# Rotary tables fetched a slot ahead, and a transpose moved in front of the next masks, in a six-layer local-attention transformer

## The chip, the cores and the metric

One Trainium2 core runs the whole program in one launch. The metric is device time in microseconds (us); the time before is a median of three runs. The profile and the trace are of one further, profiled execution. Engines: TensorE (PE; PEld is its weight load), VectorE (DVE), ScalarE (ACT), GpSimd (POOL) and SyncE (SP), which issues most DMAs.

## The reference

Four blocks in a row act on x of shape (4, 512, 128), each as `x = x + attention(layernorm(x)) * silu(ffn(layernorm(x)))`. The change lies in the "ffn" of the third block, which is itself a transformer ("the first transformer", prefix `l2`): six layers, 16 heads of 64, windows of 32 tokens.

```python
for i in range(DEPTH):                                   # 6
    x = attn_layer(shift_tokens(x), Wqkv[i], q_scale[i], k_scale[i], Wo[i]) + x
    x = ffn_layer(shift_tokens(x), ...) + x
# attn_layer
q = l2norm(q) * qs;  k = l2norm(k) * ksc
q = q * cos * scale + rotate_half(q) * sin * scale
k = k * cos * inv + rotate_half(k) * sin * inv
sim = 8 * q k^T over the own and the previous window, masked;  out = softmax(sim) v
```

## The kernel before

**Tables.** `cos*scale` and `sin*scale` do not depend on the layer, but `qs` and `ksc` do. For each layer two tables of 1 MB (i=1 for K, i=0 for Q) are fetched into one of three buffers (`tables`, L1613; DMA issued by ACT, L1617) and multiplied in place by the layer's column (two ACT scalings of 128x1024, L1620). `tables` is called where a table is first used, but neither the fetch nor the scaling is pinned, so the scheduler may move them. In the program as built, the K table of layer l+2 is fetched in the first slot of layer l+1, as soon as a buffer comes free, and its scalings stand among the GELUs of that slot on ACT's queue. The Q table of layer l+1 is fetched and scaled in the last slot of layer l.

**Slots.** Work is cut into slots: one per layer, batch row b (4) and half of the heads gp (2), so 48. In each slot three generators are merged by planned costs (the numbers that they yield): `queries_keys` for this slot (L1624), `attention` about one slot behind (L1864), `feed_forward` further behind (L1688). PE's order is then pinned to this merge order (`placed`, L128/L124 are the helpers that issue every transpose and matmul), and so are a few ACT instructions (Ln, Exp, Gelu).

**Pieces**, as PE sees them, with the names that the text uses:

- QK: two 128x512 matmuls of a projection; four per slot. Its PSUM buffer is read by ACT (square, L1650) and then by DVE (times table, L1652 and L1654); POOL adds (L1651, L1655).
- UNIT: `unit_length` (L1673), the sums of squares of K; ACT takes Ln (L1678) and Exp (L1679) in PSUM, DVE multiplies (L1681), and SP copies K into `l_qk`.
- SC: two mask matmuls and 64 small score matmuls of one unit (a pair of heads in each of four groups); DVE takes the maximum (L1788) and subtracts it into P (L1790), POOL scales P (L1792), ACT takes the exponential (L1795).
- TURN: eight transposes of P (`turn`, L1797); ACT copies the result to PT (L1804). WEIGH: 64 small matmuls of PT with V; DVE divides into On (L1833).
- BACK: eight transposes of On (`turn_back`); ACT copies them into OT (L1846). CLOSE: four matmuls of OT with Wo, cut in two halves with WEIGH between them; the second matmul reads the part of OT that the last BACK wrote. DVE adds to y (L1859).
- V: half of the values; ACT copies (L1753). LEN: small matmuls for the lengths of Q; ACT Ln and Exp (L1738, L1739).
- Feed-forward: mean, variance (L1697 to L1704), w1 with GELU (L1713), w2.

All PSUM tiles of this transformer come from one pool of four buffers; a piece waits until the buffer that it takes was read by its last user.

**Steps.** A batch row has two slots and four units. From one SC to the next is a step, and from the second layer on the four steps of a row repeat, named here by their feed-forward work. PE's order before:

```
MEAN  SC mean      BACK QK   CLOSE WEIGH CLOSE LEN TURN QK
VAR   SC variance  BACK UNIT V     WEIGH QK    V   TURN QK
W1    SC w1 (x6)   BACK QK   CLOSE WEIGH CLOSE LEN TURN QK
W2    SC           BACK UNIT V w2  WEIGH QK    V   TURN QK
```

Of the kernel before, what the change touches and what calls it, by code (L numbers as in the profile page):

```python
# [17 lines left out]
F32 = mybir.dt.float32  # L18
# [7 lines left out]
B, S, D = 4, 512, 128  # L26
# [1163 lines left out]
class _Transformer:  # L1190
# [68 lines left out]
    def tables(self, l, i):  # L1259

        if ("tab", l, i) not in self.weights:
            nc, pre = self.nc, self.pre
            tab = self.TB.tile([128, 2, 2, S], F32, name=pre + "_tab")
            nc.scalar.dma_start(tab, self.a["k_rot_" + pre][:, 4 * i : 4 * i + 4, :].rearrange("p (m h) s -> p m h s", m=2))
            for h in range(2):
                v = tab[:, :, h, :]
                nc.vector.tensor_scalar(v, v, self.col(l, 9 + 2 * i + h), None, ALU.mult)
            self.weights["tab", l, i] = tab
        return self.weights["tab", l, i]
# [328 lines left out]
class _Paired(_Transformer):  # L1598
# [11 lines left out]
        nc.sync.dma_start(hb[64:128, 1:S], y[64:128, 0 : S - 1])  # L1610
        return hb

    def tables(self, l, i):  # L1613
        if ("tab", l, i) not in self.weights:
            nc, pre = self.nc, self.pre
            tab = self.TB.tile([128, 2, 2, S], F32, name=pre + "_tab")
            nc.scalar.dma_start(tab, self.a["k_rot_" + pre][:, 4 * i : 4 * i + 4, :].rearrange("p (m h) s -> p m h s", m=2))  # L1617
            for h in range(2):
                v = tab[:, :, h, :]
                nc.scalar.mul(v, v, self.col(l, 9 + 2 * i + h))  # L1620
            self.weights["tab", l, i] = tab
        return self.weights["tab", l, i]

    def queries_keys(self, rows):  # L1624
        net, nc = self.net, self.nc
        self.shift[rows[0]] = self.moved(rows[0][1], "hb")
        late = None
        for n, (l, b) in enumerate(rows):
            hb = self.shift[l, b]
            hk = hb.rearrange("p (u s k) -> p s u k", s=2, k=self.W)  # L1630
            for gp in range(self.GP):
                w = self.part("qk", l, gp)
                if gp and n + 1 < len(rows):
                    self.shift[rows[n + 1]] = self.moved(rows[n + 1][1], "hb")
                before, made = None, {}
                for i in (1, 0):
                    tab = self.tables(l, i)
                    t = self.TP.tile([128, 2, 2, S], F32, name=self.pre + "_rot", bufs=3)
                    sums = []
                    for g in range(2):  # L1640
                        p = self.S2()
                        for h in range(2):
                            c = 128 * (4 * g + 2 * i + h)
                            o = p[:, h, :]
                            net.mm(
                                o.rearrange("p (s u k) -> p s u k", s=2, k=self.W) if i else o, w[:, c : c + 128],
                                hk if i else hb,
                            )
                        sq = self.TP.tile([128, 2, S], F32, name="sqp", bufs=4)
                        nc.scalar.activation(sq, p, AF.Square)  # L1650
                        nc.gpsimd.tensor_tensor(sq[:, 0, :], sq[:, 0, :], sq[:, 1, :], ALU.add)  # L1651
                        nc.vector.tensor_tensor(t[:, g], p, tab[:, 0], ALU.mult)  # L1652
                        m = self.TP.tile([128, 2, S], F32, name="rotp", bufs=2)
                        nc.vector.tensor_tensor(m, p, tab[:, 1], ALU.mult)  # L1654
                        nc.gpsimd.tensor_tensor(t[:, g], t[:, g], m[:, ::-1, :], ALU.add)  # L1655
                        sums.append(sq)
                        yield 1.72
                        if before:
                            made["k"] = yield from self.unit_length(*before)
                            before = None  # L1660
                    before = sums, t
                    if late:
                        yield 0.7
                        yield from self.lengths(*late)
                        late = None
                made["q"] = self.stack(t)
                self.made[l, b, gp] = made
                late = made, sums
                if gp and n + 1 == len(rows):
                    yield from self.lengths(*late)  # L1670
                yield None
# [192 lines left out]
    def attention(self, rows):  # L1864
        units = [dict(l=l, b=b, gp=gp, j=j) for l, b in rows for gp in range(2) for j in range(2)]
        yield from self.values(units[0])
        yield 5.5
        OT = None
        for i in range(len(units) + 2):
            if i % 2:  # L1870
                yield None
            u = units[i] if i < len(units) else None
            last = units[i - 1] if 0 < i <= len(units) else None
            older = units[i - 2] if i > 1 else None
            if u:
                if i % 2 == 0:
                    qk = self.made.pop((u["l"], u["b"], u["gp"]))
                else:
                    u["ve"], u["vo"] = last["ve"], last["vo"]
                self.weights_of(u, self.scores(qk, u["j"]), qk["r"])  # L1880
                yield 1.85
            if older:
                if i % 2 == 0:
                    OT = self.TP.tile([128, 4, S], F32, name=self.pre + "_OT", bufs=1)
                self.turn_back(older, OT)
            yield 0.9
            behind = iter((3.44,))
            if i % 2 == 0 and i + 2 < len(units):
                behind = self.values(units[i + 2])
            elif i % 2 and older:  # L1890
                behind = self.close(older, OT)
            yield from itertools.islice(behind, 1)
            if u:
                self.exponentials(u)
            if last:
                self.divide(last, self.weigh(last))
                yield 0.95
            yield from behind
            if u:
                self.turn(u)  # L1900
                yield 0.9


def _constants():
# [141 lines left out]
```

## Time and profile before

| what | value |
|---|---|
| median of three runs | 3774.01 us (3765.28 to 3774.3) |
| profiled execution, its time | 3785.04 us |
| profiled execution, its span | 3783.3 us |
| first transformer in the span | about 1580 to 3210 us |
| PE busy in the whole span | 3401.7 us (90%) |
| from 2100 to 2360 us: PE, DVE, ACT, POOL busy | 245.9, 180.3, 138.4, 141.0 of 260 us |

The profiled execution is 11.0 us longer than the median; sums are made in the profile and carried over as differences. A busy PE counts matmuls in flight, so idle time and the distance between starts say more than the share. In the views, "x<-y" is written tile and read tiles, a trailing "[t <-z]" is idle time and what ended it, and a line such as `ACT l_tab L1620 <- DMA ...: 24.7, 7, 5.7` is total wait, how often, longest.

### The profile page before, as it was taken

The page shows a single profiled execution, that of the slowest core. Times are in us where ns is not written, and L with a number is a line of the kernel's source. Part 1 is how long each engine was busy: PE and PEld are TensorE (multiplying, and loading weights), DVE is VectorE, ACT ScalarE, POOL GpSimd, SP SyncE. Part 2 cuts the span into 40 slices and gives each one's busy share as a digit, 9 for nine tenths or more (in the row PEclk, how much of TensorE's full clock was granted, in tenths as well). Part 3 has the DMA queues.
Part 4 walks back from the last instruction along what each step waited for, and adds up shares of the span by engine and source line. Part 5 has one row for each costly group of instructions (what it writes and reads, how often), then busy time and mean ns, then how long its engine had stood idle before and what let it go on. Part 6 is the DMA issues. An engine that isn't in the chain of part 4 may idle for free.

```text
span 3783.3 us, 108894 instructions
## 1 busy us (share of the span) xinstructions
PE 3401.7 (90%) x48517; PEld 1858.1 (49%) x48645; DVE 2187.5 (58%) x3133; ACT 1810.1 (48%) x2468; POOL 1345.3 (36%) x1136
## 2 busy tenths in 40 slices
PE   7787899989899998899999999999999999679887
PEld 4454455544444443455555555555555555445454
DVE  6675455510533533376677666676676776367764
ACT  2333566633233333455555545555555555345555
POOL 1101343400011112465555555555555553042220
PEclk7677999999989999999999999999999999889998
DMA  1000000010100000154544555445545553323221
GB/s 39 8 24 7 26 1 1 1 59 2 53 1 3 1 3 2 45 123 116 128 106 117 124 114 127 104 110 136 117 100 124 114 114 93 104 65 76 52 50 40
DMA packets 131267, 248.92 MB, mean 66 GB/s; under 512 B 31160, under 2 KB 48736, under 8 KB 123872
## 3 DMA queue, kind: packets, MB, share of 16 engines
q1 hardware_dynamic: 121744, 222.16, 24.9%
q10 hardware_dynamic: 8624, 19.29, 1.6%
q8 instruction: 384, 6.29, 0.7%
q0 software_dynamic: 432, 0.51, 0.1%
q14 instruction: 83, 0.68, 0.1%
HBM read 50.08 MB, written 5.54 MB: 15 GB/s over the span
## 4 chain that ended last, share of the span: by engine, by line
PE 63%; DVE 14%; ACT 11%; issue 7%; DMA 3%; POOL 2%; SPq 0%; POOLq 0%; DVEq 0%; ACTq 0%
PE S L124 42%; PE S L128 6%; PE M L124 5%; PE o L1113 4%; ACT l_P L588 3%; PE o L621 2%; DVE l_rot L1652 1%; DVE rotp L1654 1%; DMA l_tab<-in_k_rot_l 1%; ACT sqp L1650 1%; PE S L1023 1%; DVE l_P L1790 1%; DVE mx L1788 1%; DVE l_mx L1088 1%; ACT l_P L1135 1%
## 5 line engine op out<-in xcount | busy, mean ns | idle before, releaser
L1655 POOL TENSOR_TENSOR l_rot<-l_rot,rotp 128x1024 f32<-128x1024 f32 x192 | 452.5, 2357 | 174.5 <-DVE rotp L1654 166.8
L124 PE MATMUL S<-hb,l_wqk 128*128 128x512 f32 x896 | 439.8, 610 | 25.3 <-DVE hb L92 9.8
L1651 POOL TENSOR_TENSOR sqp<-sqp 128x512 f32<-128x512 f32 x192 | 245.3, 1278 | 488.9 <-ACT sqp L1650 480.1
L1652 DVE TENSOR_TENSOR l_rot<-S,l_tab 128x1024 f32<-128x1024 f32 x192 | 234.5, 1221 | 295.8 <-ACT sqp L1650 290.9
L128 PE MATMUL S<-core,l_P 128*128 128x128 f32 x1856 | 265.2, 288 | 40.5 <-ACT l_P L1437 16.5
L128 PEld LDWEIGHTS S<-core,l_P 128*128 128x128 f32 x1856 | 216.2, 146 | 135.9 <-issue 46.4
L124 PE MATMUL S<-l_KT,l_QT 32*128 32x256 f32 (+7 forms) x1536 | 250.3, 480 | 33.8 <-ACT l_P L1135 14.2
L1135 ACT ACTIVATE l_P<-S 128x1024 f32<-128x1024 f32 x160 | 156.7, 1022 | 258.3 <-PE S L124 258.3
L1139 POOL TENSOR_SCALAR_AFFINE_SELECT l_P<-l_P 128x256 f32<-128x256 f32 x256 | 99.4, 406 | 407.6 <-ACT l_P L1135 403.3
L1650 ACT ACTIVATE sqp<-S 128x1024 f32<-128x1024 f32 x192 | 196.3, 1023 | 95.6 <-PE S L124 92.8
L124 PE MATMUL S<-l_OT,l_wo 128*128 128x512 f32 (+1 forms) x512 | 224.0, 562 | 18.7 <-DVE ffu L1584 7.7
L1654 DVE TENSOR_TENSOR rotp<-S,l_tab 128x1024 f32<-128x1024 f32 x192 | 233.0, 1214 | 0.7 <-POOL l_rot L1655 0.7
L124 PE MATMUL S<-l_wv,hb 128*128 128x512 f32 x448 | 217.0, 607 | 15.7 <-DVE l_rot L1681 7.1
L124 PEld LDWEIGHTS S<-hb,l_wqk 128*128 128x128 f32 x896 | 154.4, 192 | 151.7 <-issue 119.1
L1088 DVE TENSOR_REDUCE l_mx<-S 128x2 f32<-128x768 f32 (+1 forms) x192 | 154.9, 863 | 126.3 <-PE S L1023 126.3
L124 PEld LDWEIGHTS S<-l_ve,l_PT 64*32 64x32 f32 (+1 forms) x6656 | 159.9, 108 | 96.4 <-issue 54.9
L124 PE MATMUL S<-l_vo,l_PT 64*32 64x64 f32 (+1 forms) x6656 | 187.6, 226 | 5.8 <-issue 5.8
L1792 POOL TENSOR_TENSOR l_P<-l_P,rq 128x1024 f32<-128x1024 f32 x96 | 182.6, 1902 | 27.9 <-DMA xT<-away_x 14.2
L124 PE MATMUL S<-l_ve,l_PT 64*32 64x64 f32 (+1 forms) x6656 | 184.8, 226 | 8.4 <-issue 7.5
L124 PE MATMUL S<-l_qk 64*32 64x64 f32 x12288 | 152.5, 226 | 34.1 <-issue 16.5
L1681 DVE SCALAR_TENSOR_TENSOR l_rot<-S,l_rot 128x1024 f32<-128x1024 f32 x96 | 113.1, 1219 | 101.9 <-ACT S L1679 97.8
L124 PEld LDWEIGHTS S<-l_qk 64*32 64x32 f32 x12288 | 132.7, 105 | 65.1 <-issue 58.7
(406 smaller groups left out, 6785.8 us busy)
## 6 DMA issues: line engine op xcount, KB each, us to landing
l_qk<-l_rot SPq DMA_DIRECT2D x896, 128.0 KB
l_ve<-l_vo SPq DMA_DIRECT2D x160, 256.0 KB
l_tab<-in_k_rot_l ACTq DMA_DIRECT2D x16, 1024.0 KB
l_ve<-l_vo SPq DMA_DIRECT2D x48, 192.0 KB
l_wqk<-in_l2Wqkv SPq DMA_DIRECT2D x12, 512.0 KB
l_wv<-in_l2Wqkv SPq DMA_DIRECT2D x12, 256.0 KB
l_wo<-in_l2Wo SPq DMA_DIRECT2D x12, 256.0 KB
hb<-xn SPq DMA_DIRECT2D x24, 128.0 KB
```

The source lines that it names most:

```text
L124: self.placed(self.nc.tensor.matmul(out, lhsT, rhs, start=start, stop=stop, **kw))
L128: self.placed(self.nc.tensor.transpose(out, in_, self.ident[:n, :n]))
L588: nc.scalar.activation(P[:, e, c : c + n], P[:, e, c : c + n], AF.Exp, bias=mn[:, i : i + 1], scale=-1.0, accum_out=rs[:, i : i + 1],)
L1088: nc.vector.tensor_reduce(mxv[:, bs, 2 * m + e, 3 - i], s[u][:, :, c : c + n], axis=AX.X, op=ALU.max)
L1113: nc.tensor.matmul(o[b // 2][x : x + 32, S - n : S], V[:, 4 * (m // 2) + i, 32 * b : 32 * b + 32], P[b // 2][:, b % 2, c : c + n], start=i ...
L1135: nc.scalar.activation(P[u], s[u], AF.Exp, scale=scale)
L1650: nc.scalar.activation(sq, p, AF.Square)
L1651: nc.gpsimd.tensor_tensor(sq[:, 0, :], sq[:, 0, :], sq[:, 1, :], ALU.add)
L1652: nc.vector.tensor_tensor(t[:, g], p, tab[:, 0], ALU.mult)
L1654: nc.vector.tensor_tensor(m, p, tab[:, 1], ALU.mult)
L1655: nc.gpsimd.tensor_tensor(t[:, g], t[:, g], m[:, ::-1, :], ALU.add)
L1792: nc.gpsimd.tensor_tensor(P, P, rq.unsqueeze(2).to_broadcast([128, 16, 64]), ALU.mult)
```

## The change

`tables` becomes `fetch` and `adapt`, both pinned to program order on ACT. The K table of layer l+1 is fetched at the start of slot (l, b=2, gp=1) and scaled at the start of (l, 3, 1); the Q table is fetched in (l, 3, 1) between the K and Q projections and scaled in (l+1, 0, 0) at the same point. In `attention`, `turn` of a unit no longer stands at the end of its own step, but directly in front of the next unit's masks, and its planned cost is added to the one of the scores.

```diff
-    def tables(self, l, i):
-        if ("tab", l, i) not in self.weights:
...
-            nc.scalar.dma_start(tab, self.a["k_rot_" + pre][:, 4 * i : 4 * i + 4, :].rearrange("p (m h) s -> p m h s", m=2))
-            for h in range(2):
-                v = tab[:, :, h, :]
-                nc.scalar.mul(v, v, self.col(l, 9 + 2 * i + h))
...
+    def fetch(self, l, i):
+        tab = self.TB.tile([128, 2, 2, S], F32, name=self.pre + "_tab")
...
+        self.net.placed(self.nc.scalar.dma_start(tab, src))
+    def adapt(self, l, i):
+        for h in range(2):
+            v = self.weights["tab", l, i][:, :, h, :]
+            self.net.placed(self.nc.scalar.mul(v, v, self.col(l, 9 + 2 * i + h)))
...
+                ahead = gp and l < rows[-1][0]
+                if ahead and b == B - 2:
+                    self.fetch(l + 1, 1)
+                if ahead and b == B - 1:
+                    self.adapt(l + 1, 1)
                 for i in (1, 0):
-                    tab = self.tables(l, i)
+                    if i == 0 and l and (b, gp) == (0, 0):
+                        self.adapt(l, 0)
+                    if i == 0 and ahead and b == B - 1:
+                        self.fetch(l + 1, 0)
+                    tab = self.weights["tab", l, i]
...
-        yield 5.5
+        yield 6.4
...
+                if last:
+                    self.turn(last)
                 self.weights_of(u, self.scores(qk, u["j"]), qk["r"])
-                yield 1.85
+            elif last:
+                self.turn(last)
+            yield 2.75
...
             yield from behind
-            if u:
-                self.turn(u)
-                yield 0.9
```

Since the costs that the merge sees are other ones, more than TURN moves. PE's order after, as the program is built:

```
MEAN  SC mean      QK   BACK CLOSE WEIGH CLOSE LEN   QK TURN
VAR   SC variance  UNIT BACK V     QK    WEIGH V     QK TURN
W1    SC w1 (x6)   QK   BACK CLOSE WEIGH CLOSE LEN   QK TURN
W2    SC           UNIT BACK w2 V  QK    WEIGH V     QK TURN
```

On ACT the square of the QK in front of BACK now stands ahead of the copy of OT, and UNIT's Ln, the copy of OT and UNIT's Exp follow each other in that order.

## The prediction

> **What bounds the kernel.** I read the page's engine shares first, then the windows of single steps in the first transformer, then what PE and ACT waited for there, and last the chain of waits and ACT's timeline at the places that the diff touches.
>
> ```profile
> span 3783.3 us, 108894 instructions
> PE 3401.7 (90%) x48517; PEld 1858.1 (49%) x48645; DVE 2187.5 (58%) x3133; ACT 1810.1 (48%) x2468; POOL 1345.3 (36%) x1136
> ```
>
> PE is the busiest engine by far. The next view has one step per line: start and end, length, busy time of PE, PEld, DVE, ACT, POOL, granted clock, DMA share, GB/s. They are MEAN, W1 at the first slot of a layer, VAR, an ordinary W1, and W2.
>
> ```profile
> 2047.00:2061.60 14.60, 14.04 (x356) 8.26 (x356) 10.23 (x12) 6.47 (x9) 11.31 (x7) 1.00 0.82 203
> 2078.60:2101.90 23.30, 20.60 (x366) 10.81 (x366) 12.40 (x17) 12.02 (x14) 11.82 (x8) 0.93 0.66 165
> 2134.60:2150.90 16.30, 15.16 (x296) 8.32 (x296) 12.16 (x12) 10.87 (x12) 6.89 (x5) 1.00 0.18 42
> 2150.90:2169.30 18.40, 18.25 (x367) 10.20 (x367) 12.45 (x17) 10.06 (x12) 11.84 (x8) 1.00 0.61 138
> 2169.30:2185.80 16.50, 16.35 (x301) 9.25 (x301) 12.65 (x13) 8.94 (x9) 7.18 (x5) 1.00 0.44 101
> ```
>
> An ordinary row takes 14.6 + 16.3 + 18.4 + 16.5 = 65.8 us, and PE is nearly always in work. W1 and W2 have PE idle for 0.15 us: whatever new wait falls there is paid in full. The W1 at the first slot of a layer is 4.9 us longer. What ended PE's idle times in the repeating part (1805 to 3137 us; total, times, longest), and the chain inside that long step (start, length, what):
>
> ```profile
> PE S L124 <- issue: 22.6, 34, 1.4
> PE S L124 <- DVE l_P L1790: 12.9, 32, 0.4
> PE S L124 <- DVE ffg L1714: 7.9, 4, 2.5
> PE S L124 <- DVE l_rot L1681: 6.2, 11, 0.6
> PE S L124 <- ACT l_OT L1846: 1.8, 2, 0.9
> ```
> ```profile
> 2078.67 7.09 DMA l_tab<-in_k_rot_l
> 2085.79 1.15 ACT l_tab L1620
> 2086.96 1.28 ACT L1713
> 2088.25 0.70 ACT ffg L1713
> 2088.97 0.76 DVE ffg L1714
> 2089.78 9.21 PE S L124 x147
> ```
>
> ACT stands at the scaling until the table has landed 7.09 us after its issue; the last GELU queues behind it, the gated product L1714 behind that, and PE waits for a PSUM buffer.
>
> **Part 1, the tables.** The fetch is now a slot (about 33 us) ahead of the scaling, so this wait goes. By step lengths: W1 at the first slot of layers 1 to 4 took 22.79, 23.36, 22.03 and 22.28 us against 18.32 in a quiet row, 17.2 us too much. VAR at the last slot of five layers, where the Q table was fetched and scaled, took 18.90, 16.97, 16.61, 17.31, 16.97 against 16.38, 4.9 too much. Together 22.0 us. Bounds: 17.2 if VAR's excess has other causes, and 30.6, all of DVE's idle time that ended with a table's DMA. What is late next in these steps is only what stands in the other rows.
>
> The four scalings (1.15 us each) per layer remain. K's pair, 2.3 us, is now ahead of the square in one MEAN step per layer; there ACT is busy for 6.5 of 14.6 us, and the CLOSE behind it waits anyway by part 2, so only about 0.1 us is left: 5 x 0.1 = 0.5 (with no cover 2.3 each, 11.5). Q's pair lies in a W2 step, where ACT has 7.6 us to spare: 0.
>
> The K fetch now meets a MEAN step with DMA share 0.82. Before, it lay in a step with 0.66. The fetch is waited for a slot later, but other transfers share its engines: the copies of Q that the next scores need, and PE's instructions, since the 34 waits on "issue" (22.6 us, 0.66 each) are PE waiting for no engine. Bounds: 0 if these copies' slack of some 5 us holds, and 10 if each of the five fetches adds three such gaps (5 x 3 x 0.66). Taken: 3.
>
> [...] No row of before has a table fetch in a MEAN step.
>
> **Part 2, the order.** I replay each step with the durations of one quiet slot (starts to next starts on PE: QK and V 1.72, BACK and TURN 0.9, one CLOSE matmul 0.86, UNIT, w1 and w2 as before). ACT at the end of w1, before:
>
> ```profile
> 2976.21 0.68 ACT L1713 ACTIVATE ffg<-S,l_cols 85x512 f32<-85x512 f32 x1 [1.03 <-PE S L124]
> 2976.91 1.28 ACT L1285 ACT_TABLE_LOAD   x1
> 2978.20 1.01 ACT L1846 COPY l_OT<-S 128x1024 f32<-128x1024 f32 x1
> 2979.11 1.03 ACT L1650 ACTIVATE sqp<-S 128x1024 f32<-128x1024 f32 x1
> ```
>
> PE's w1 ended at 2976.01. GELU, table load and the copy of OT ran while PE did BACK and QK, and CLOSE did not wait. Four steps, with t=0 at the end of the step's feed-forward work:
>
> - **W1.** PE does QK until 1.72, BACK until 2.6, CLOSE's first matmul until 3.46. ACT is ready at 2978.20, so 2.19; the square now comes first and the copy of OT starts 0.91 later, at 3.10, and ends at 4.11. With 0.15 to resume, CLOSE's second matmul starts at 4.26: 0.8 us of new wait. ACT then does the exponential L1795, which has time. 21 rows have it: +16.8.
> - **MEAN.** QK ends at 0; the square starts at 0.2, the copy of OT at 1.11 and ends at 2.12. PE: BACK until 0.9, CLOSE's first matmul until 1.76, second at 2.27: 0.5 of wait. In return the wait of CLOSE for DVE's L1790 goes (12.9 us, 32 times, 0.40 each), since more PE work now lies between the subtraction and the reuse of its buffer. Net 0 (-0.1 to +0.1 a row).
> - **W2.** The order of PSUM buffers changes. The second-last QK takes the buffer of the QK only three tiles back. DVE frees it 3.53 us after that QK's end (square 0.2, L1652 at 1.26, L1654 until 3.53) plus 0.15; WEIGH entered from QK and V take 1.57 + 1.82 = 3.39. Wait 0.3: 21 x 0.3 = +6.3. With a third user of the same kind the wait would be a whole 1.2; with V's copy earlier, 0.
> - **VAR.** This step is a locked chain from the end of the QK in front of its masks (t=0, 3018.3 in the slot below): DVE's two table products end at 3.53, maximum and subtraction at 6.0, the feed-forward's parts (L1704) at 7.4, then Ln, Exp, and L1681, whose end at 11.86 lets the second V start:
>
> ```profile
> 3025.66 1.07 ACT L1678 ACTIVATE S<-S,l_tiny 128x1024 f32<-128x1024 f32 x1
> 3026.76 1.01 ACT L1679 ACTIVATE S<-S 128x1024 f32<-128x1024 f32 x1
> ```
> ```profile
> 3027.80 2.36 DVE L1681 SCALAR_TENSOR_TENSOR l_rot<-S,l_rot 128x1024 f32<-128x1024 f32 x2 [2.89 <-ACT S L1679]
> ```
>
>   Before, V started at 11.99 and V, TURN and QK (1.72 + 0.9 + 1.72) followed: 16.3. After, OT's copy (0.91) stands between Ln and Exp, so V starts at 12.9, and V, QK and TURN follow until 17.2; but the masks at the step's start come 0.9 after t=0, since a TURN stands there too: 16.3 again, net 0. If the chain doesn't begin early, because the SC that DVE waits for now comes behind that TURN, it costs 0.9 x 21 = +19; if the wait for L1681 (6.2 us in all) went, -6.
> - **TURN** in front of the masks needs the exponential L1795 of the unit behind, done long before. It has no row in this place; the nearest are TURN in front of QK (0.93 against 0.87 elsewhere) and WEIGH, which costs 0.16 when entered from wide matmuls. Bounds 0 and 0.16 x 84 = 13; taken 0, since TURN's count and neighbours of 128 columns stay.
> - **Rows of the first layer without feed-forward** (3): about 0.8 each, +2.4.
>
> **Sum.** -22.0 + 0.5 + 3 + 16.8 + 0 + 6.3 + 0 + 2.4 = +7.0 us. The profiled execution would be 3785.04 + 7 = 3792, and the median, which is 11.0 lower, 3774.0 + 7 = 3781.
>
> **Rivals.**
>
> *The copy of OT is late in all 48 CLOSE passages (slower).* If ACT reaches the square late everywhere, CLOSE's second matmul waits for a square and a copy less one matmul: 1.01 + 1.02 - 0.86 = 1.17. 48 x 1.17 = 56, less 12.9 for L1790, plus 6.3 for W2, less 22: +27, so 3801. It decides as soon as OT's copy ends more than 0.86 us after BACK. For it: the two waits that PE already had for L1846 (0.9 at most). Against: in MEAN ACT is idle for more than half.
>
> *The new waits are hidden (faster).* If the scheduler's order leaves ACT ready before QK ends, or if the waits eat idle time that PE had anyway ("issue", 22.6 us), only the tables remain: 3774 - 22 = 3752; with the waits for L1790 and L1681 gone too (12.9 + 6.2), 3733. For it: both are real rows. Against: W1 has no idle time that could swallow 0.8.
>
> *The change does not do what it says* (no gain from tables, as the scheduler brings them together again): fetch and scaling are both pinned, some 40 ACT instructions apart, so I leave it out.
>
> **How the numbers follow.** The forecast has 0.55, the slower rival 0.20, the faster 0.25. A measurement here can tell about 0.3%, 11.3 us, so "same" is 3763 to 3785. The forecast's own spread (3766 to 3796, from the table's bounds, the fetch's 0 to 10, and W2's and TURN's ends) lies 0.33 in same, 0.20 above and 0.02 below. The slower rival gives 0.18 to slower and 0.02 to same, the faster 0.23 to faster and 0.02 to same. Faster 0.25, same 0.37, slower 0.38. The range 3752 to 3804 leaves out the faster rival's lower half (about 0.12) and the slower rival's upper part (0.08).
>
> **What would show it.** Right: ACT's wait for the table's DMA is gone; W1 at a layer's first slot falls to about 19.1 like all others; a new row "PE <- ACT l_OT" of about 0.8 in W1 and 0.5 in MEAN; W2 at 16.8, VAR at 16.4, MEAN at 14.6; the row for L1790 gone. Wrong: W1 stays at 18.3, or VAR grows by the 0.9, or "issue" rises in the MEAN steps with a fetch.

## The result, and the profile after

The changed kernel takes 3805.6 us (median of five, 3801.9 to 3815.05) against 3774.3 of the kernel before in the same series: ratio 1.0085, 95% interval 1.006 to 1.011. It is slower by 31 us, where +7 was forecast, and 1.6 us beyond the end of the range. The two profiled executions lie 27.2 us apart (spans 3810.5 and 3783.3).

The page of the changed kernel shows hardly more PE work in a longer span, at the same share:

```profile
span 3810.5 us, 108883 instructions
PE 3421.3 (90%) x48645; PEld 1864.7 (49%) x48645; DVE 2202.4 (58%) x3133; ACT 1798.2 (47%) x2470; POOL 1347.8 (35%) x1136
```

The windows of single steps of the changed kernel, in the columns of before (start and end, length, PE, PEld, DVE, ACT, POOL busy, granted clock, DMA share, GB/s): an ordinary MEAN, VAR, W1 and W2, the W1 at the first slot of a layer, and a MEAN with a K fetch.

```profile
3028.00:3042.70 14.70, 14.42 (x358) 8.45 (x356) 10.41 (x12) 6.01 (x9) 9.40 (x6) 1.00 0.69 151
3042.70:3059.00 16.30, 14.86 (x298) 8.57 (x296) 12.17 (x12) 10.66 (x13) 9.01 (x6) 1.00 0.18 41
3059.00:3078.10 19.10, 18.54 (x368) 10.05 (x367) 12.83 (x17) 9.97 (x13) 9.81 (x8) 1.00 0.64 142
3010.90:3028.00 17.10, 16.93 (x303) 9.37 (x301) 12.66 (x13) 8.79 (x10) 9.18 (x5) 1.00 0.40 93
2093.70:2113.50 19.80, 18.95 (x369) 10.24 (x368) 12.82 (x17) 11.35 (x15) 9.81 (x8) 1.00 0.71 157
1706.10:1729.50 23.40, 17.46 (x359) 9.51 (x357) 10.43 (x12) 6.07 (x9) 9.35 (x6) 0.85 0.62 145
```

The first three lines are the forecast almost to the digit: 14.7, 16.3, 19.1. W2 is 17.1 where 16.8 was forecast. The fifth is 3.5 us shorter than its counterpart of before. The last was not forecast: PE is idle for 6 of 23.4 us, and the granted clock is 0.85. The same step took 16.7 us before.

What ended PE's idle times in the repeating part of the changed kernel (total, times, longest):

```profile
PE S L124 <- DVE l_rot L1694: 26.1, 20, 1.4
PE S L124 <- issue: 24.8, 27, 2.6
PE S L124 <- ACT l_OT L1859: 15.7, 36, 0.6
PE S L124 <- DVE rotp L1667: 2.3, 11, 0.2
```

The old row for P's subtraction (12.9 us) is nearly gone, as is ACT's wait of 24.7 us for the table's DMA. New are OT's copy (L1859), UNIT's product L1694, for which V waits in the locked VAR, and L1667, which frees the PSUM buffer of W2's last QK.

A step can be laid beside its twin of before, since both kernels have the same 94 steps in the same order. Step lengths (start of masks to start of the next masks), summed by kind from the two traces:

| steps | count | before | after | difference | forecast |
|---|---|---|---|---|---|
| MEAN with the K fetch | 5 | 77.7 | 92.2 | +14.5 | +3 |
| other MEAN (five with K's scaling) | 17 | 258.2 | 258.4 | +0.2 | +0.5 |
| VAR at the last slot of a layer | 5 | 86.8 | 86.3 | -0.5 | -4.9 |
| other VAR | 17 | 278.0 | 276.4 | -1.7 | 0 |
| W1 at the first slot of a layer, and other W1 | 22 | 424.5 | 426.3 | +1.8 | -17.2 + 16.8 |
| W2 | 21 | 356.5 | 365.0 | +8.5 | +6.3 |
| steps without feed-forward | 7 | 101.5 | 104.2 | +2.7 | +2.4 |
| until the first step | | 1599.6 | 1601.9 | +2.3 | 0 |

The last row is no effect of the change: in the kernels below the first step began anywhere from 1590.1 to 1602.3 us. The rest sums to +25.5, 18.5 above the forecast: 11.5 of it in the MEAN steps with the K fetch, 2.7 in VAR, 2.2 each in W1 and W2.

**What the long MEAN steps wait for.** Step by step they took 23.4, 19.2, 15.9, 18.1 and 15.6 us. In the first of them ACT issues the K table at 1703.19; the trace's table packets run from 1704.29 to 1709.41. PE's timeline in the changed kernel then has this line (idle before it and what ended it in brackets):

```profile
1712.76 0.44 PE L124 MATMUL S<-l_qk 64*32 64x64 f32 x8 [4.64 <-issue]
```

"issue" says that no engine released PE. The DMA queues of the changed kernel say what was missing; first from 1704.2 to 1709.9, then from 1709.9 to 1712.8 us (packets, MB, share of 16 engines; q10 carries the table, q1 the copies that SP issues):

```profile
q10 hardware_dynamic: 144, 1.05, 67.4%
q1 hardware_dynamic: 240, 0.39, 31.3%
```
```profile
q1 hardware_dynamic: 239, 0.68, 107.0%
q8 instruction: 1, 0.02, 2.9%
```

While the table moves, no packet of q8 runs; this queue, of the kind "instruction" and with packets of 16 KB, is taken for PE's by the pattern that follows. The next one starts at 1710.01, 0.6 us after the table's last, ends at 1711.36, and PE goes on 1.40 us later. In none of the five steps does a q8 packet begin during the K table's transfer (4.4 to 5.2 us), and none of PE's idle times over 0.1 us there ends with a copy's landing. That PE goes on behind a q8 packet is a pattern: in all 70 waits on "issue" over 0.4 us in the transformer in the two traces, PE went on between 1.21 and 1.71 us after the end of a q8 packet (medians 1.39 and 1.43).

The gap is then paid twice, since the granted clock behind it is 0.50. The window right after it in the changed kernel:

```profile
1713.10:1718.40 5.30, 5.30 (x10) 2.08 (x7) 2.45 (x2) 0.60 (x1) 0.00 (x0) 0.50 1.02 217
```

At a granted clock of 0.50 the QK there takes 3.41 us where it takes 1.72 elsewhere.

**POOL's order in the same steps.** Not all of the 14.5 us is the transfer's. POOL is not pinned, and in these five slots, in the changed kernel alone of all kernels here, the sum of squares (L1664) stands ahead of P's scaling (L1805). In the third of the steps:

```profile
2276.13 1.27 POOL L1664 TENSOR_TENSOR sqp<-sqp 128x512 f32<-128x512 f32 x1 [0.80 <-ACT sqp L1663]
2277.36 1.90 POOL L1805 TENSOR_TENSOR l_P<-l_P,rq 128x1024 f32<-128x1024 f32 x1
```
```profile
2283.45 1.02 PE L124 MATMUL S<-hb,l_wqk 128*128 128x512 f32 x2 [1.25 <-DVE l_On L1846]
```

In the other MEAN steps P's scaling comes first: it starts 5.3 us into a quiet step, and 7.2 us into this one. So the exponential, DVE's division L1846 and with it the PSUM buffer of the last QK come later. This step has no wait on "issue" over 0.1 us; its excess is this wait. Three of the five steps have it (1.06, 1.25 and 0.33 us), 2.6 us in all.

### The profile page after: what moved, and what is told of

It reads as the page before. It is cut to its first block, busy times and chain, and to the rows that moved or that the text cites. A ratio compares the mean times of both kernels' runs of the same rounds, so it can differ in the third digit from the quotient of the medians.

```text
span 3810.5 us, 108883 instructions
## 1 busy us (share of the span) xinstructions
PE 3421.3 (90%) x48645; PEld 1864.7 (49%) x48645; DVE 2202.4 (58%) x3133; ACT 1798.2 (47%) x2470; POOL 1347.8 (35%) x1136
## 3 DMA queue, kind: packets, MB, share of 16 engines
q1 hardware_dynamic: 121744, 222.16, 24.7%
## 4 chain that ended last, share of the span: by engine, by line
PE 62%; ACT 14%; DVE 13%; issue 7%; POOL 2%; DMA 2%; SPq 1%; POOLq 0%; ACTq 0%; DVEq 0%
PE S L124 42%; PE M L124 5%; PE S L128 4%; PE o L1113 4%; ACT l_P L588 3%; PE o L621 2%; ACT sqp L1663 2%; ACT l_OT L1859 2%; DVE l_rot L1694 1%; DVE l_rot L1665 1%; DVE rotp L1667 1%; PE S L1023 1%; DVE l_mx L1088 1%; ACT l_P L1135 1%; DVE mx L1801 1%
## 5 line engine op out<-in xcount | busy, mean ns | idle before, releaser
L1664 POOL TENSOR_TENSOR sqp<-sqp 128x512 f32<-128x512 f32 x192 | 245.7, 1280 | 410.2 <-ACT sqp L1663 395.4
L128 PE MATMUL S<-core,l_P 128*128 128x128 f32 x1856 | 262.6, 286 | 38.9 <-ACT l_P L1437 16.7
L124 PE MATMUL S<-l_KT,l_QT 32*128 32x256 f32 (+7 forms) x1536 | 250.9, 481 | 34.2 <-ACT l_P L1135 14.5
L124 PEld LDWEIGHTS S<-hb,l_wqk 128*128 128x128 f32 x896 | 164.8, 193 | 216.8 <-issue 177.1
L124 PE MATMUL S<-l_OT,l_wo 128*128 128x512 f32 (+1 forms) x512 | 233.9, 569 | 33.0 <-ACT l_OT L1859 22.6
L1667 DVE TENSOR_TENSOR rotp<-S,l_tab 128x1024 f32<-128x1024 f32 x192 | 233.3, 1215 | 0.8 <-POOL l_rot L1668 0.8
L1805 POOL TENSOR_TENSOR l_P<-l_P,rq 128x1024 f32<-128x1024 f32 x96 | 182.5, 1901 | 39.9 <-DVE l_P L1803 31.1
L1694 DVE SCALAR_TENSOR_TENSOR l_rot<-S,l_rot 128x1024 f32<-128x1024 f32 x96 | 113.2, 1220 | 126.7 <-ACT S L1692 125.5
L124 PEld LDWEIGHTS S<-l_vo,l_PT 64*32 64x32 f32 (+1 forms) x6656 | 158.5, 107 | 16.6 <-issue 16.5
```

What stands on the lines that cost most here:

```text
L124: self.placed(self.nc.tensor.matmul(out, lhsT, rhs, start=start, stop=stop, **kw))
L128: self.placed(self.nc.tensor.transpose(out, in_, self.ident[:n, :n]))
L1694: nc.vector.scalar_tensor_tensor(t[:, g], p[:, g, :].unsqueeze(1).to_broadcast([128, 2, S]), 1e12, t[:, g], ALU.min, ALU.mult)
L1805: nc.gpsimd.tensor_tensor(P, P, rq.unsqueeze(2).to_broadcast([128, 16, 64]), ALU.mult)
```

## The experiments

Ratios are to the kernel before on the same chip. Step sums of each kernel's trace stand in the table at the end of this section. In all of them theory A is that the K fetch in MEAN delays PE's instructions and that the order has its own price; the rivals are named in the expectations.

**Tables alone and order alone.** Each is one half of the diff: `tables_only` has `fetch` and `adapt` with the attention of before, `order_only` the new attention with the tables of before.

> The new fetch and adapt, with the old attention (TURN at the end of its step, old costs). Theory A (the K fetch in the MEAN step keeps PE's instructions waiting there, and the order has its own cost): the W1 steps at layers' first slots lose 4 us each (about -17), VAR about -1 to -5, but the MEAN steps with a fetch still grow by about 14 in all: 3768 us (3760 to 3776). Rival B (the long MEAN steps come from the new order, not from the fetch): no long MEAN steps here, 3753 us.

> The new attention (TURN in front of the masks, costs 6.4 and 2.75), with the old tables. Theory A: W1 +0.87 and W2 +0.55 in each of about 21 rows (30), early steps +3, VAR -1: 3806 us, and no MEAN step over 17 us. Rival B (long MEAN steps belong to the order): 3820 us, with the long MEAN steps at some layers. If the order costs nothing, 3774.

Measured: `tables_only` 3785.2 us, ratio 1.0011 (0.9996 to 1.0026); `order_only` 3802.4 us, 1.0063 (1.0042 to 1.0083). The long MEAN steps are in `tables_only` (20.5, 17.0, 16.7, 16.2, 18.3) and none is in `order_only` (14.7 to 15.7): rival B falls. `tables_only` does shorten the first W1 steps by 15.8 us; 11 of it is given back in the MEAN steps with the fetch. Theory A explains only a part of these 11: in each of the five PE's QK waits 1.10 us for OT's copy (5.5 us), which it does there neither before nor in `tables_later`; two of them have 6.8 and 3.4 us at a clock of 0.50; the waits on "issue" are 4.8 us in sum, as before (4.7). The time also missed the 3760 to 3776 that was expected, since VAR gave back only 0.9 us and K's scaling costs 1.0 us in each of its five MEAN steps (15.7 where a quiet one takes 14.66): with the old order PE's QK waits 1.05 to 1.21 us there for L1667, whose square stands behind the scaling on ACT. The order costs 24 us, 8 less than I had expected: W1 and W2 are as long as expected, but its first W1 steps, still with the old tables, are 5.9 shorter than before (20 to 21 us instead of 22 to 23). The new order hides part of the old wait, so the halves don't add up in the first W1 steps. In the medians they do within the noise (4 and 24 us against 31).

**The K fetch half a slot later.**

```diff
-                if ahead and b == B - 2:
-                    self.fetch(l + 1, 1)
...
                 for i in (1, 0):
+                    if i == 0 and ahead and b == B - 2:
+                        self.fetch(l + 1, 1)
```

> The changed kernel, but the K fetch is issued in front of the Q projections of the same slot, which is at the end of the MEAN step, so that it lands in VAR, where the DMA share was 0.18. Theory A: the MEAN steps with a fetch fall back to about 15.3 us, 14 in all, VAR pays 0 to 3: 3793 us. Rival C (the issue gaps wander and have nothing to do with the fetch): unchanged, 3805 us.

Measured: 3794.6 us, ratio 1.0039 (1.0027 to 1.0052), 0.46% or 17 us less than the changed kernel. The five MEAN steps fell from 92.2 to 75.0, and the other VAR steps paid 3.7 in sum. The same step as above, in this kernel:

```profile
1704.30:1720.60 16.30, 14.67 (x359) 8.41 (x357) 10.58 (x12) 5.95 (x9) 9.40 (x6) 1.00 0.66 148
```

It is 16.3 us instead of 23.4, at full clock. Rival C, gaps that wander without cause, falls.

**A dose.** The fetch is cut in two halves, one for each 32 columns of a head (cosines and sines of both), the second in front of the Q projections.

```diff
+        if l and i:
+            self.net.placed(self.nc.scalar.dma_start(tab[:, :, 0, :], src[:, :, 0, :]))
+            self.rest = tab, src
...
+                    if i == 0 and ahead and b == B - 2:
+                        tab, src = self.rest
+                        self.net.placed(self.nc.scalar.dma_start(tab[:, :, 1, :], src[:, :, 1, :]))
```

> The changed kernel, the K fetch cut in two: half of the table at the start of the slot, the other half in front of the Q projections. A dose: if PE's instructions wait behind the table's packets for as long as these last, half the bytes cost half, MEAN steps with a fetch 85 us instead of 92.2, 3799 us; if there is a slack that half a table fits into, they fall to 75 and the time to 3792; if the place or the issue on ACT costs, not the bytes, 3806.

Measured: 3799.7 us, ratio 1.0048 (1.003 to 1.0065). The MEAN steps take 92.2 with the whole table, 79.8 with half of it, 75.0 with none: half the bytes cost 28% of the excess. So it is not the issue on ACT, which still stands there; but as a dose this is rough. All of it lies in two of the five steps (19.1 and 16.2), POOL's order is the usual one again here and in `fetch_later`, which alone takes 2.6 us off, and the interval of the time overlaps that of `fetch_later` and that of the changed kernel.

**BACK ahead of QK again.** The total of the planned costs stays; TURN stays in front of the masks.

```diff
-            yield 2.75
+            yield 1.85
...
                 self.turn_back(older, OT)
-            yield 0.9
+            yield 1.8
```

> The changed kernel with the same total of planned costs, 0.9 of it moved from in front of BACK to behind it, so that PE does BACK ahead of QK and UNIT again and ACT copies OT ahead of the square; TURN stays in front of the masks. Theory A: the waits for OT's copy (18.8 us in the trace) go, W1 falls to about 18.4, and since the copy no longer stands between Ln and Exp the second V of VAR starts 0.9 earlier, VAR 15.4: together -38, 3768 us; with VAR unchanged 3787. Rival (the copy is not what CLOSE waits for, or another release is as late): 3805 us.

Measured: 3768.1 us, ratio 0.9972 (0.9953 to 0.999), against 1.0085 for the changed kernel: 1.13% or some 43 us less, as the two spans have it too (3766.7 and 3810.5; 39.5 of it from the first step on). PE's order is the new one, but with BACK in front of QK and UNIT. ACT at the end of w1, first in the changed kernel with what PE did for it, then in `back_first`:

```profile
3067.12 1.28 ACT L1285 ACT_TABLE_LOAD   x1
3068.41 1.02 ACT L1663 ACTIVATE sqp<-S 128x1024 f32<-128x1024 f32 x1
3069.33 1.01 ACT L1859 COPY l_OT<-S 128x1024 f32<-128x1024 f32 x1
```
```profile
3070.39 1.12 PE L124 MATMUL S<-l_OT,l_wo 128*128 128x512 f32 x2 [0.56 <-ACT l_OT L1859]
```
```profile
2960.71 1.01 ACT L1859 COPY l_OT<-S 128x1024 f32<-128x1024 f32 x1
2961.62 1.03 ACT L1663 ACTIVATE sqp<-S 128x1024 f32<-128x1024 f32 x1
```

In the changed kernel OT's copy follows the square and CLOSE's second matmul stands for it; with the copy first, CLOSE ran through. The windows of a VAR and a W1 step in `back_first`:

```profile
2935.70:2951.20 15.50, 14.91 (x298) 8.61 (x297) 12.16 (x12) 10.83 (x13) 8.98 (x5) 1.00 0.19 44
2951.20:2969.60 18.40, 18.40 (x369) 10.25 (x368) 12.65 (x17) 10.00 (x13) 9.85 (x9) 1.00 0.62 139
```

W1 is back at 18.4, and VAR fell from 16.3 to 15.5: its chain is shorter now that no copy stands between Ln and Exp, while TURN's move lets it begin early. W2 (372.8 in all) became longer still: a quiet one takes 17.0 (17.1 in the changed kernel), but PE met more waits on "issue" (gaps over 0.06 us in the trace: 14.9 us in W2 against 8.1). The K fetch is still in the MEAN steps, 90.4 us.

**The two cures together, and no fetch at all.** `both` is `back_first` with the fetch of `fetch_later`. `no_fetch` is `back_first` in which layer l+1's table is scaled out of layer l's, by the quotient of the two columns.

```diff
-            v = self.weights["tab", l, i][:, :, h, :]
-            self.net.placed(self.nc.scalar.mul(v, v, self.col(l, 9 + 2 * i + h)))
+            c = self.ratio[:, l - 1, 2 * i + h : 2 * i + h + 1] if l else self.col(l, 9 + 2 * i + h)
+            self.net.placed(self.nc.scalar.mul(tab[:, :, h, :], old[:, :, h, :], c))
```

> back_first (0.9 of the planned cost behind BACK) with the K fetch at the end of the MEAN step as in fetch_later. Theory A: the five MEAN steps with a fetch, 90.4 us in back_first, fall to about 75, VAR pays 0 to 3: 3753 us, 15 below back_first (3768). Rival C (issue gaps wander): 3768.

> back_first without any table fetch after the first: each layer's table is scaled out of the layer's before, by the quotient of the two columns (ten quotients more at the start; the scales must not be zero). Theory A: MEAN steps as in both, and VAR at the last slots loses the 1.6 us that one Q fetch took: 3751 us. If the fetches cost nothing wherever they stand: as back_first, 3768.

Measured: `both` 3759.5 us, ratio 0.9941 (0.9921 to 0.9961); `no_fetch` 3750.2 us, 0.9917 (0.989 to 0.9944). The MEAN steps are 74.9 and 74.0. `back_first` and `both` are the cleanest pair for the fetch, since in these steps both have P's scaling first on POOL and OT's copy ahead of the square on ACT. Of the 15.5 us between them, the waits on "issue" make 8.9 (12.4 against 3.5); the rest is, as an estimate, half of the 13.2 us that `back_first` runs there at a clock of 0.50, with none in `both`, since the QK above took 3.41 us instead of 1.72 at that clock. The times of the two overlap in their intervals, and 3753 had been expected of `both`. In `both` two VAR steps at last slots still take 19.6 and 19.2, with the Q fetch issued in front of them; in `no_fetch` all five take 15.5 or 15.6. Both beat the kernel before and the changed one.

**The old order with the later fetch.**

> tables_only (old attention) with the K fetch at the end of the MEAN step. Theory A: MEAN steps with a fetch fall from 88.8 to about 76, the first W1 steps keep their gain of 16: 3771 us. If the whole gain of 22 that the prediction gave to the tables is there: 3756. If the fetch costs as much in VAR: 3785.

Measured: 3768.9 us, ratio 0.9968 (0.9952 to 0.9985). The tables alone, well placed, bring 12 us, not 22: the first W1 steps gain 15.5, the five MEAN steps with K's scaling lose 3.7 (1.0 each against a quiet one), and VAR at the last slots gains 2.1.

Step sums in us, worked out as above:

| kernel | MEAN, K fetch (5) | VAR, last slot (5) | W1, first slot (5) | other W1 (17) | W2 (21) | other VAR (17) |
|---|---|---|---|---|---|---|
| before | 77.7 | 86.8 | 108.8 | 315.7 | 356.5 | 278.0 |
| after | 92.2 | 86.3 | 97.8 | 328.5 | 365.0 | 276.4 |
| `tables_only` | 88.8 | 85.9 | 93.0 | 314.9 | 358.3 | 277.6 |
| `tables_later` | 75.8 | 84.7 | 93.3 | 316.4 | 359.2 | 278.2 |
| `order_only` | 76.6 | 90.7 | 102.9 | 328.1 | 364.2 | 276.6 |
| `fetch_split` | 79.8 | 87.4 | 98.7 | 328.3 | 367.8 | 277.3 |
| `fetch_later` | 75.0 | 84.7 | 96.7 | 328.3 | 365.6 | 280.1 |
| `back_first` | 90.4 | 79.2 | 94.5 | 315.2 | 372.8 | 263.9 |
| `both` | 74.9 | 85.4 | 94.6 | 318.4 | 371.6 | 266.4 |
| `no_fetch` | 74.0 | 77.7 | 93.3 | 315.6 | 370.1 | 263.0 |

## Why the prediction was wrong, step by step

- **The replayed order was right.** W1's new wait for OT's copy was put at 0.8 us, and a quiet W1 is 0.87 longer; `back_first`, which puts BACK in front of QK and with it OT's copy ahead of the square again, takes it away. MEAN at no change measured +0.01 a step. VAR at 16.3 with the second V waiting for L1694 is in this line of the changed kernel:

```profile
3054.64 1.53 PE L124 MATMUL S<-l_wv,hb 128*128 128x512 f32 x3 [1.44 <-DVE l_rot L1694]
```

- **The step that failed is the K fetch's cost, taken at 3 with an upper bound of 10.** It measured 14.5 in the changed kernel's trace, and `fetch_later` got 17 back. In these steps the waits on "issue" rose from 4.7 to 10.8 us, two of them ran for 6.8 and 3.4 us at a clock of 0.50, and 2.6 us are POOL's order, of which the prediction had nothing. It had named the sign, "issue" rising in the MEAN steps with a fetch, but not its price: even the upper bound of 10 leaves the sum at +14. The bound was made of three gaps of 0.66 us per fetch, the mean of gaps that arise without a fetch. With a fetch the gap was not one more of these: in none of the five steps did a q8 packet begin before the table's 4.4 to 5.2 us of packets were through, PE was idle for 4.64 us in the worst step, and the clock was 0.50 behind the wait in two of the five. I had both rows, DMA share 0.82 and the waits on "issue", and priced the second as if the first left its size alone. That no row of before has a table fetch in a MEAN step was misread as well: the five Q tables landed at the ends of MEAN steps, in the one shown (2047.0 to 2061.6) from 2057.19 to 2061.01, and these steps took 14.7 to 15.3 us. The K table now moves at the start of a MEAN step.
- **VAR's 4.9 us of the tables' gain did not come (-0.5), though the wait went.** Before, in the first of the five, ACT waited 1.90 us for the Q table and PE 2.04 us for L1654 behind it; that is gone, and three of the five now take 16.3 us like any other VAR. But the Q fetch is still issued in front of this step, and in the other two PE waited 2.7 and 2.6 us on "issue". In `no_fetch` all five are as short as the rest, while `back_first` still pays in one (17.05) and `both` in two. So the transfer took back what the moved scaling had saved.
- **The 17.2 us of the first W1 steps came almost whole:** 15.8 in `tables_only`, 15.5 in `tables_later`. The upper bound of 30.6 beside it was misread, as it is no idle time of DVE in this transformer: 24.7 us of it are ACT's waits at L1620, and 5.9 are DVE's at L1267, which runs from 3266 us on, behind this transformer. K's scaling, taken at 0.5 in all, cost 1.0 in each of its five steps with the old order. In the changed kernel these five steps are 2.1 us longer than before in sum (76.8 against 74.6), and two of them hold waits on "issue" of 1.24 and 0.99.
- **W2 was put at +0.3 and measured +0.55 in a quiet step, +0.40 in the mean of 21.** The wait for the PSUM buffer was the right one: QK started 0.44 late behind the last V (2.16 instead of 1.72 from start to start), with 0.1 more in the transitions of the new neighbours. Over 21 steps (+8.5 for +6.3) this is 2.2 us of the miss.
- **The slower rival was near the measured time (3801) for another reason.** PE waited 18.7 us for OT's copy in the whole transformer, 42 times with 0.45 in the mean, not 56 us with 1.17 each. The faster rival fell with W1's and W2's waits.
- **PE's instructions were rightly named among the traffic that a fetch meets.** They come in q8 packets of 16 KB, 384 of them in the changed kernel's span, and the wait for them is not hidden: PE waited 38.7 us on "issue" in the changed kernel's transformer (33.7 before).

What stays open: the five steps with a fetch lie 8.2, 4.0, 0.8, 3.0 and 0.5 us above the median of the other MEAN steps, 15.15. In the first and the fourth the next q8 packet began 0.6 and 1.0 us behind the table's last packet. In the second it began 3.2 us behind it, with other transfers on the engines (share 1.06), and the waits ended 6 and 11 us behind the table, so that the table's part in them is argued, not shown. The third is POOL's order. The runs don't let me place a fetch between two of these packets. That the longer W2 of `back_first` is this queue too is read from its waits, and no run isolates it.

## What to carry to other kernels

A prefetch that takes the wait off one engine's queue still has to find a stretch where its bytes don't delay anybody: look at the DMA share of the step that it moves into, and count PE's own instructions among the traffic there, with the length of the transfer as the price that a step may pay (4.64 us in one step here, nothing in another), not the size of today's gaps. Compare the built order of the engines that are not pinned as well. When an order changes, replay which of two results an engine delivers first: putting BACK, and with it OT's copy, ahead again was worth some 43 us here, more than the tables. And an excess beside a transfer may be the transfer's own: only moving or removing the bytes tells it from the wait.

## What the runs showed of the hardware

PE's instruction packets were held back while a table moved. In eight traces (all but `fetch_split` and `no_fetch`), between 1640 and 3160 us, 78 whole tables were fetched, in 4.3 us each in the mean; 61 packets of q8 began meanwhile, and 39 of these in the last 0.6 us of a transfer. In the traces before and after alone it is 19 tables (3.7 to 5.8 us each), 11 packets and 8 of them in the last 0.6 us. These two have 464 q8 packets in the whole stretch, one in 6.6 us; at that rate 11 would have begun in the earlier part of the 19 transfers, where 3 did, and 2 in their last 0.6 us. In the 70 waits above PE went on about 1.4 us after such a packet ended.

In the traces before and after, every change of the granted clock but the first lies within 0.01 us of a grid of 3.41 us. Two stretches of this grid in the kernel before:

```profile
1790.49:1793.90 3.41, 1.36 (x5) 0.68 (x4) 3.38 (x4) 2.83 (x4) 2.37 (x2) 1.00 0.77 200
1793.90:1797.31 3.41, 3.41 (x5) 1.18 (x4) 1.65 (x2) 1.72 (x2) 2.99 (x2) 0.50 0.31 121
```

PE is idle for 2.05 us of the first, and the next one runs at 0.50. In all ten traces between 1640 and 3160 us, each of the 18 stretches at full clock with 1.84 us or more of PE idle was followed by 0.50, for one stretch or two; of those with less only two were (1.73 and 1.33 us), and one with 1.79 was not. In the traces before and after, the stretches that were followed by 0.50 had 2.05, 2.08, 2.34, 3.41 and 1.33 us of PE idle. After the idle 4.64 us the clock was 0.50 until 1718.61; the 2.71 us of a VAR step lay across two stretches, with 1.79 us in one of them, and the clock stayed at 1.00. Why the 0.50 came behind 1.33 us of idle, in the second MEAN step with a fetch, no run shows.
